# Two evictions of a four-layer model on one core: Delta's second bank from ScalarE to VectorE, and VectorE first at the shared scores bank

## The chip, the cores and the metric

The kernel runs on one core of a Trainium2 chip. The metric is the device time of one execution in microseconds (us), here the median of three. Lower is better. The profile is of one further execution with its own time.

Engines: TensorE (PE, with its weight loads PEld), VectorE (DVE), ScalarE (ACT), GpSimd (POOL) and SyncE (SP), which issues nearly all DMAs. Each has its own queue of instructions.

## The reference

The input is a batch of 8 images of 56 x 56 positions and 192 channels. Four layers follow each other, each as `x = x + layer(group_norm(x))`:

```python
# layer 0: gated Toeplitz mixing along both axes, 576 channels
out = p * (toeplitz_w(q * v, a1) + toeplitz_h(q * v, a2)) @ o_w.T + o_b
# layer 1: 7 x 7 window attention, shifted by 3, 6 heads of 32
attn = softmax((q * hd**-0.5) @ k.T + bias + mask);  out = (attn @ v) @ proj_w.T + proj_b
# layer 2: depthwise 3 x 3 convolution
# layer 3: selective scan over 4 directions, 384 channels, 16 states
delta = softplus(dts + dt_b)
dA = exp(delta * A);  dBu = delta * u * B
h[t] = dA[t] * h[t-1] + dBu[t];  y[t] = sum_n h[t] * C[t] + D * u[t]
```

In layer 3 two directions run along rows (forward and backward) and two along columns. The four results are added, normed over the channels, gated with silu(z) and projected back.

## The kernel before

**Three parts.** The first (to L300) computes the Toeplitz products of all images. The second runs the *front* of image 0 beside the rest of the first. A front is everything from the gate of layer 0 to the deltas of layer 3 of one image, in five stages: `gate` (L448), `attention`, `conv2`, `inner`, `steps`. In the first two parts the instructions are placed by the framework's scheduler. The third part is the scan loop, under a manual schedule: the order in which the program writes the instructions is the order in the queues. It holds the scans of all images and the fronts of images 1 to 7.

**The scan loop.** An image is cut into chunks of 448 positions, 7 for each of the 4 directions, so 28. A chunk has 3 blocks of 128 channels and 8 groups of 2 states, so an image has 28 x 24 = 672 *pairs* (block and group), and the loop runs over 5376 of them. A pair consists of: `inject` (L1059, GpSimd: delta * u times B), `decay` (L1076, ScalarE: two exponentials into a PSUM tile of which there are two), `initial` (L1066) and `keep_state` (L1098, small ScalarE copies), `scan` (L1085, VectorE), `times_c` (L1091, on GpSimd for even groups, on VectorE for odd ones) and `add_up` (L1106, TensorE sums over the states in PSUM). After the last group of a block `sums` (L1116, L1118, VectorE) adds the result to `ysum`. Once the fourth direction has passed a chunk, `finish` (L959 to L1003) norms, gates and projects it.

**Fronts and `finish` beside the scans.** Both are generators. Each `yield` ends a *segment* and tells the planner how many PSUM banks are held across it, how many the next one needs, and sometimes a delay. There are two such banks. After each pair the loop calls `parts.step`, which may resume each generator several times, up to limits. The planner keeps a planned time per engine and adds the cost of every instruction as it writes it. Front costs were logged while image 0's front was written: `Meter` (L46) gives each instruction a base and a cost per element: 0.2 + 0.83e-3 n us on ScalarE, 0.1 + 1.05e-3 n on VectorE, 0.04 + 1.25e-3 n on TensorE; the costs of a segment count one after the other. `Parts.fits` decides whether a segment goes now:

```python
t, at, grace = dict(self.t), entry.ready, 3.0 * entry.waits
for engine, cost in entry.costs[entry.at]:
    if engine == "D" and at > t["D"] + limit["D"] + grace:
        return False
    at = t[engine] = max(t[engine], at) + cost
return all(t[e] <= max(limit[e] + grace, self.t[e]) for e in "AE")
```

The limit of "D" (VectorE) in the loop is 0.2 us. A refusal adds one to `entry.waits`, an admission sets it to 0.

**The deadline.** A chunk's deltas are loaded ahead of it: at block 1, group 0 of the chunk before, which is 16 pairs ahead of the chunk's first pair. For the first chunk of image b these deltas come from image b's own front, so the loop there says

```python
while (b1, slot1 // 2, j1) not in made:
    parts.step(anything, ahead_of)
```

with no limits, until `steps` has made the block. The next front is added as soon as the one before is through.

**The stages that the change touches or that matter here.** In `attention` the loop runs over 8 rows of windows and in each over 4 groups `q` of two windows. For each group: the scores of the six heads in three banks of 196 columns (L614); the third of these banks also takes the product v (L643), 192 columns behind the scores. `biased` (the call lands on L619, VectorE) scales the scores and adds the bias. `nc.scalar.copy(v, pv)` (L645) takes v out of the shared bank. Then the row maximum (L648, VectorE), the exponentials (L651, ScalarE, in two segments of three), the reciprocal (L656, VectorE), the scaling (L659, ScalarE), transposes (L666) and the product with v (L678).

In `inner`, for each of 3 blocks of 128 channels: for 7 tiles a projection with two halves (L840), evicted by ScalarE (L845, L848), one half going to a padded buffer in DRAM; from it the convolution (loads L811, matmuls L869, evictions L879); Silu of both halves over the whole image (L886, with the reload of z's half at L883 and the stores at L888); seven ScalarE copies that turn rows into columns (L892), and a store (L896).

In `steps`, for each direction axis o (columns first) and each of 7 chunks: load (L907), matmul (L918), a ScalarE copy (L920), then for each of 3 blocks two matmuls (L928) into two banks, one bank for each of the two directions s, and their evictions with the bias (L933, ScalarE, 128 x 448); at the end the Softplus of all six at once (L937, 128 x 2688) with a table load ahead of it and one behind it, and the stores (L940).

Of the kernel before, what the change touches and what calls it, by code (L numbers as in the profile page):

```python
# [16 lines left out]
AF = mybir.ActivationFunctionType  # L17
ALU = mybir.AluOpType
# [9 lines left out]
CH = 448  # L28
# [60 lines left out]
def model(ctx: ExitStack, tc: tile.TileContext, a: dict, out: bass.AP):  # L89
    nc = tc.nc  # L90
# [213 lines left out]
    with (  # L304
# [4 lines left out]
        cb2, cb3, dt_b = (load_const(wp, n) for n in ("cb2", "cb3", "dt_b"))  # L309
# [34 lines left out]
        def bank():  # L344
            return ps.tile([128, 512], F32, name="ps_f")
# [6 lines left out]
        bias, bmask, masks = carve(slab, PT_, (NH, WS, 2, WS), (4, 6, PT_), (4, PT_))  # L352
# [175 lines left out]
        def attention(b):  # L528
# [40 lines left out]
            p = bank()  # L569
# [11 lines left out]
            for wh in range(H // WS):  # L581
                x = xs[:, wh % 2]
                yield 0, 0

                for k in range(2):
                    nc.scalar.copy(x[:, k, :, W:], x[:, k, :, :SHIFT])

                    nc.scalar.copy(
                        xw[:, k].rearrange("p q (i j) -> p q i j", i=WS),
                        x[:, k, :, SHIFT:].rearrange("p i (q j) -> p q i j", q=4),  # L590
                    )
                for m in range(4):
                    yield 0, 1
                    p = bank()
                    for k in range(2):
                        nc.tensor.matmul(
                            p[:CP, :n],
                            w_qkv[:, k, m * CP : (m + 1) * CP],
                            xw[:, k].rearrange("p q t -> p (q t)"),
                            start=k == 0,  # L600
                            stop=k == 1,
                        )
                    yield 1, 0
                    nc.scalar.activation(
                        qk[:, m].rearrange("p q t -> p (q t)"), p[:CP, :n], AF.Identity, bias=nb[:CP, m : m + 1]
                    )
                if wh + 1 < H // WS:
                    load_x(wh + 1)
                for q in range(4):
                    kind = 2 * (wh == 7) + (q == 3)  # L610

                    def scores(p, hh, t):
                        row = slice(hh * HD, (hh + 1) * HD)
                        nc.tensor.matmul(  # L614
                            p[:PT_, t * PT_ : (t + 1) * PT_], qk[row, t, q, :], qk[row, 2 + t, q, :], start=True, stop=True
                        )

                    def biased(p, hh):
                        nc.vector.scalar_tensor_tensor(  # L619
                            S[:, 2 * hh : 2 * hh + 2, :],  # L620
                            p[:PT_, : 2 * PT_].rearrange("p (t m) -> p t m", t=2),
                            HD**-0.5,
                            bmask[:, kind, 2 * hh : 2 * hh + 2, :],
                            ALU.mult,
                            ALU.add,
                        )


                    yield 0, 2
                    p0, p1 = bank(), bank()  # L630
                    for t in range(2):
                        scores(p0, 0, t)
                        scores(p1, 1, t)
                    yield 2, 0
                    biased(p0, 0)
                    biased(p1, 1)
                    yield 0, 1
                    p = bank()
                    for t in range(2):
                        scores(p, 2, t)  # L640
                    pv = p[:PT_, 2 * PT_ : 2 * PT_ + C]
                    for k in range(2):
                        nc.tensor.matmul(pv, xw[:, k, q, :], w_qkv[:, k, 2 * C :], start=k == 0, stop=k == 1)  # L643
                    yield 1, 0
                    nc.scalar.copy(v, pv)  # L645
                    biased(p, 2)
                    mx, sm = mxs[:, 0], mxs[:, 1]
                    nc.vector.tensor_reduce(mx, S, axis=AX.X, op=ALU.max, negate=True)  # L648
                    yield 0, 0
                    for e in range(6):  # L650
                        nc.scalar.activation(  # L651
                            S[:, e, :], S[:, e, :], AF.Exp, bias=mx[:, e : e + 1], accum_out=sm[:, e : e + 1]
                        )
                        if e == 2:
                            yield 0, 0
                    nc.vector.reciprocal(sm, sm)  # L656
                    yield 0, 0
                    for e in range(6):
                        nc.scalar.activation(S[:, e, :], S[:, e, :], AF.Copy, scale=sm[:, e : e + 1])  # L659
                        if e == 2:  # L660
                            yield 0, 0
                    for g in range(2):
                        yield 0, 1
                        p = bank()
                        for e in range(3):
                            nc.tensor.transpose(  # L666
                                p[:PT_, e * PT_ : (e + 1) * PT_], S[:, 3 * g + e, :], ident[:PT_, :PT_]
                            )
                        yield 1, 0
                        nc.scalar.copy(  # L670
                            ST[:, 3 * g : 3 * g + 3, :].rearrange("p a m -> p (a m)"), p[:PT_, : 3 * PT_]
                        )
                    yield 0, 1
                    p = bank()
                    for t in range(2):
                        for hh in range(3):
                            h = 3 * t + hh
                            nc.tensor.matmul(  # L678
                                p[hh * HD : (hh + 1) * HD, t * PT_ : (t + 1) * PT_],
                                v[:, h * HD : (h + 1) * HD],  # L680
                                ST[:, 2 * hh + t, :],
                                start=True,
                                stop=True,
                            )
                    yield 1, 0
                    nc.scalar.copy(oT[:, :, q, :], p[:CP, : 2 * PT_].rearrange("p (t m) -> p t m", t=2))
                for m in range(2):
                    yield 0, 1
                    p = bank()
                    for t in range(2):  # L690
                        nc.tensor.matmul(
                            p[:CP, :n],
                            w_pr[:, t, m * CP : (m + 1) * CP],
                            oT[:, t].rearrange("p q (i j) -> p i q j", i=WS),
                            start=t == 0,
                            stop=t == 1,
                        )
                    yield 1, 0
                    pi = p[:CP, :n].rearrange("p (h w) -> p h w", h=WS)
                    for cd, cs in ((slice(0, W - SHIFT), slice(SHIFT, W)), (slice(W - SHIFT, W), slice(0, SHIFT))):  # L700
                        nc.vector.scalar_tensor_tensor(
                            x[:, m, :, cs], pi[:, :, cd], vb[:, m : m + 1], x[:, m, :, cs], ALU.add, ALU.add
                        )
                for i0, i1, h0 in rows(wh):
                    for k in range(2):
                        nc.sync.dma_start(out=image(x2_d[b], k, i0, i1, h0), in_=x[:, k, i0:i1, :W])
# [192 lines left out]
        def steps(b):  # L899

            w_x, xc, rc, dl = carve(slab, 128, (2, ND, 128), (2, ND, CH), (2, CH), (2, ND, CH))
# [9 lines left out]
            for n, (o, j) in enumerate(todo):  # L911
# [4 lines left out]
                p = bank()  # L916
# [5 lines left out]
                for d in range(ND):  # L922
                    yield 0, 2
                    held = []
                    for s in range(2):
                        row = slice(32 * s, 32 * s + R)
                        held.append(bank())
                        nc.tensor.matmul(  # L928
                            held[s][:, :CH], w_dt[row, o, d * 128 : (d + 1) * 128], rc[row, n % 2, :], start=True, stop=True
                        )  # L930
                    yield 2, 0
                    for s in range(2):
                        nc.scalar.activation(  # L933
                            dl[:, s, d, :], held[s][:, :CH], AF.Identity, bias=dt_b[:, 2 * o + s, d : d + 1]
                        )
                yield 0, 0
                nc.scalar.activation(dl, dl, AF.Softplus)  # L937
                usual_functions()
# [487 lines left out]
```

## Time and profile before

| | |
|---|---|
| time, median of 3 runs | 21470.86 us (21421.38 to 21477.67) |
| the profiled execution's own time | 21510.71 us |
| its span, first to last instruction | 21508.5 us |
| busy share of the span | PE 81%, DVE 73%, POOL 70%, ACT 58% |
| first scan of the loop (L1085) | 3423.3 us |
| granted TensorE clock, mean | 0.865 |
| L645 (v out of the shared bank) | 224 in the loop, 319 ns median |
| L933 (delta's evictions) | 588 in the loop |

The page tells busy time by engine, then the span in 40 slices. Up to slice 6 (3423 us) the first two parts run; from there on the loop. The groups by line tell busy time, the mean duration of one instruction and the idle time ahead of them with what ended it. "Windows" gives the same busy time for stretches of the span, or the time and count of a single line in them; as each pair has one scan, that count is the number of pairs. Instructions written for image 0's front and placed by the scheduler all carry the line of the recording helper (L83), so the counts by line of the front's stages are those of images 1 to 7.

### The profile page before, as it was taken

To read this page: it belongs to the slowest core of one execution; us is meant where nothing else is said; L and a number is where in the kernel's file an instruction comes from. 1 tells how busy PE (TensorE), PEld (TensorE's weight loads), DVE (VectorE), ACT (ScalarE), POOL (GpSimd) and SP (SyncE) were. 2 spreads that over 40 slices of the span, in tenths; PEclk is the share of its full clock that TensorE was granted. 3 is DMA by queue.
4 is the path that set the end of the run, shared out by engine and by line. 5 is a ranking of instruction groups with operands and counts; after the bars stand their busy time and mean duration, and the time that the engine had idled before them with its cause. 6 is when DMAs were issued, how large, how long until landed. Compare 5 with 4: busy or idle time off the path is not lost. (4 is left out here: it accounts for less than half of the span.)

```text
span 21508.5 us, 203992 instructions
## 1 busy us (share of the span) xinstructions
PE 17461.0 (81%) x59404; PEld 9086.2 (42%) x59404; DVE 15779.7 (73%) x12469; ACT 12490.5 (58%) x31833; POOL 15095.0 (70%) x9176
## 2 busy tenths in 40 slices
PE   7878678887887789877987788879877888787777
PEld 4845455433443344433543354334433443333333
DVE  2122116996799668977898779867987789789998
ACT  3126113666666566757575657666666667575555
POOL 0000005887788678867897778878887788689999
PEclk9587757998998889888998899889988999888888
DMA  3931676456544755466545654565446554754444
GB/s 88 248 97 39 190 211 181 131 159 213 172 142 134 217 166 152 134 183 199 160 128 172 209 157 138 159 212 170 140 148 214 173 146 132 218 180 147 134 131 128
DMA packets 2566532, 3470.45 MB, mean 161 GB/s; under 512 B 936270, under 2 KB 2518704, under 8 KB 2534578
## 3 DMA queue, kind: packets, MB, share of 16 engines
q1 hardware_dynamic: 2542724, 3340.61, 52.4%
q0 software_dynamic: 15520, 116.14, 1.5%
q8 instruction: 473, 7.75, 0.2%
q14 instruction: 647, 5.30, 0.1%
q10 hardware_dynamic: 7168, 0.65, 0.0%
HBM read 2822.68 MB, written 634.11 MB: 161 GB/s over the span
## 5 line engine op out<-in xcount | busy, mean ns | idle before, releaser
L1106 PE MATMUL ps_y<-hc,ident_sb 128*128 128x448 f32 x21504 | 10003.9, 603 | 828.4 <-POOL hc L1091 750.6
L1059 POOL TENSOR_TENSOR ring<-du,bm 128x896 f32<-128x896 f32 x5376 | 9450.8, 1775 | 745.8 <-ACT ring L1066 383.2
L1076 ACT ACTIVATE ps_a<-delta,A_logs_sb 128x449 f32<-128x449 f32 x10752 | 6859.6, 638 | 354.3 <-DVE ring L1085 97.7
L1106 PEld LDWEIGHTS ps_y<-hc,ident_sb 128*128 128x128 f32 x21504 | 4315.8, 210 | 5154.2 <-issue 3636.4
L1091 POOL TENSOR_TENSOR hc<-ring,cm 128x896 f32<-128x896 f32 x2688 | 4769.2, 1774 | 1930.7 <-DVE ring L1085 922.1
L1085 DVE TENSOR_TENSOR_SCAN ps_a<-ps_a,ring 128x898 f32<-128x898 f32 x2688 | 5428.3, 2019 | 607.8 <-ACT ps_a L1076 558.2
L1085 DVE TENSOR_TENSOR_SCAN ring<-ps_a,ring 128x898 f32<-128x898 f32 x2688 | 5424.1, 2018 | 571.8 <-ACT ps_a L1076 407.1
L1091 DVE TENSOR_TENSOR hc<-ps_a,cm 128x896 f32<-128x896 f32 x2688 | 2935.2, 1092 | 1037.6 <-PE ps_y L1106 808.0
L1098 ACT COPY state<-ps_a 128x2 f32<-128x2 f32 x2687 | 426.5, 159 | 2783.3 <-DVE hc L1091 2775.4
L287 DVE COPY tzx<-ps_tz 112x448 f32<-112x448 f32 x432 | 269.9, 625 | 1442.5 <-PE ps_tz L281 1292.4
L281 PE MATMUL ps_tz<-tzx,tm 112*112 112x112 f32 x4608 | 1031.1, 406 | 344.7 <-DMA tm<-ext 295.9
L295 POOL DMA_DIRECT2D o<-tzx x192 | 97.3, 513 | 1579.6 <-DVE tzx L287 1341.0
L281 PEld LDWEIGHTS ps_tz<-tzx,tm 112*112 112x112 f32 x4608 | 1021.8, 319 | 385.7 <-issue 381.9
L1066 ACT COPY ring<-state 128x2 f32<-128x2 f32 x4608 | 823.0, 179 | 532.2 <-POOL hc L1091 531.1
L666 PE MATMUL ps_f<-ident_sb,slab 98*98 98x98 f32 x1344 | 336.5, 325 | 602.9 <-ACT slab L659 602.7
L1098 ACT COPY state<-ring 128x2 f32<-128x2 f32 x2688 | 504.1, 188 | 489.6 <-DVE ring L1085 476.2
L1042 POOL TENSOR_TENSOR du<-delta,xcd 128x448 f32<-128x448 f32 x672 | 659.8, 982 | 20.0 <-DMA slab<-in_w_p_dram 19.6
L83 PE MATMUL ps_f<-slab 96*32 96x448 f32 (+7 forms) x2432 | 588.4, 548 | 75.9 <-DMA slab<-pad 55.9
L234 PE MATMUL ps_qv<-wqv,xn 96*128 96x384 f32 (+1 forms) x1200 | 530.3, 525 | 135.6 <-ACT sl L236 68.0
L666 PEld LDWEIGHTS ps_f<-ident_sb,slab 98*98 98x98 f32 x1344 | 202.5, 157 | 1017.5 <-ACT slab L659 798.5
L503 PE MATMUL ps_f<-ident_sb,slab 112*96 112x112 f32 x4704 | 534.7, 268 | 99.7 <-DVE slab L511 49.8
L503 PEld LDWEIGHTS ps_f<-ident_sb,slab 112*96 112x96 f32 x4704 | 513.1, 170 | 239.0 <-issue 121.6
(221 smaller groups left out, 16398.9 us busy)
## 6 DMA issues: line engine op xcount, KB each, us to landing
bm<-bc SPq DMA_DIRECT2D x1792, 448.0 KB
cm<-bc SPq DMA_DIRECT2D x1792, 448.0 KB
xcd<-xc SPq DMA_DIRECT2D x840, 224.0 KB
dl<-slab SPq DMA_DIRECT2D x224, 672.0 KB
delta<-dl SPq DMA_DIRECT2D x224, 672.0 KB
slab<-pad SPq DMA_DIRECT2D x504, 232.0 KB
tzx<-qv SPq DMA_DIRECT2D x192, 588.0 KB
o<-tzx POOLq DMA_DIRECT2D x192, 588.0 KB, 14.2
```

The costliest lines, as they stand in the source:

```text
L83: return f(*args, **kw)
L281: nc.tensor.matmul(po[:, c, :], t[:, :, c2 + c], x[:, :, c1 + c2 + c], start=True, stop=True)
L503: nc.tensor.matmul(p[:CP, t * TT : (t + 1) * TT], ot[:, n % 2, i, t, c % 2 * CP : c % 2 * CP + CP], ident[:TT, :TT], start=i == 0, stop=i ...
L666: nc.tensor.transpose(p[:PT_, e * PT_ : (e + 1) * PT_], S[:, 3 * g + e, :], ident[:PT_, :PT_])
L1042: nc.gpsimd.tensor_mul(du[:, 0, :], deltas[i][:, d, 1 : CH + 1], xcs.pop((i, d)))
L1059: nc.gpsimd.tensor_mul(hs[:, :, tokens(i)[0]], dus[i, d].to_broadcast([128, NG, CH]), bms[i, k])
L1066: nc.scalar.copy(in_ring(g)[:, :, tokens(i)[1]], src)
L1076: nc.scalar.activation(dA[:, n, :], deltas[i][:, d, at : at + CH + 1], AF.Exp, scale=negA[:, slot, d, c : c + 1])
L1085: nc.vector.tensor_tensor_scan(h, dA, hs, 0.0, ALU.mult, ALU.add)
L1091: (nc.gpsimd if on_pool(d, k) else nc.vector).tensor_mul(hc, h[:, :, tokens(i)[0]], cms[i, k])
L1098: nc.scalar.copy(states[i][:, d, NG * k : NG * k + NG], h[:, :, tokens(i)[2]])
L1106: nc.tensor.matmul(yps[i, d][:, :CH], ident, hcs[g][:, n, :], start=k + n == 0, stop=k + n == NP + NG - 2)
```

## The change

In `attention` the copy of v and the third call of `biased` change places: VectorE now reads the shared bank first, then ScalarE, then VectorE reduces. In `steps` the loop over the two directions is written out: the first direction's bank is still evicted by ScalarE (now L932), the second one's by VectorE with `tensor_scalar` (L933), which adds the bias as a scalar per partition. Over 8 images that is 336 evictions in 112 blocks of 3. No buffer, DMA or matmul is changed. The costs that `Meter` logs change with the instructions, and so do the decisions of the planner and of the scheduler ahead of the loop.

```diff
@@ -642,8 +642,8 @@
                     for k in range(2):
                         nc.tensor.matmul(pv, xw[:, k, q, :], w_qkv[:, k, 2 * C :], start=k == 0, stop=k == 1)
                     yield 1, 0
+                    biased(p, 2)
                     nc.scalar.copy(v, pv)
-                    biased(p, 2)
                     mx, sm = mxs[:, 0], mxs[:, 1]
                     nc.vector.tensor_reduce(mx, S, axis=AX.X, op=ALU.max, negate=True)
                     yield 0, 0
@@ -929,10 +929,10 @@
                             held[s][:, :CH], w_dt[row, o, d * 128 : (d + 1) * 128], rc[row, n % 2, :], start=True, stop=True
                         )
                     yield 2, 0
-                    for s in range(2):
-                        nc.scalar.activation(
-                            dl[:, s, d, :], held[s][:, :CH], AF.Identity, bias=dt_b[:, 2 * o + s, d : d + 1]
-                        )
+                    nc.scalar.activation(dl[:, 0, d, :], held[0][:, :CH], AF.Identity, bias=dt_b[:, 2 * o, d : d + 1])
+                    nc.vector.tensor_scalar(
+                        dl[:, 1, d, :], held[1][:, :CH], dt_b[:, 2 * o + 1, d : d + 1], None, ALU.add
+                    )
                 yield 0, 0
                 nc.scalar.activation(dl, dl, AF.Softplus)
                 usual_functions()
```

## The prediction

> **What bounds the kernel now.** The page's chain of work is useless here (every share is 0%), so I read the table of windows, the windows of the scan line alone (L1085, whose count is the number of pairs), the waits of VectorE, the groups by line, and the timeline of ScalarE and SyncE at one place.
>
> ```profile
> 20000.00:21000.00 1000.00, 731.85 (x1476) 315.33 (x1477) 957.23 (x602) 557.65 (x1479) 998.81 (x600) 0.86 0.43 140
> 8411.00:9198.00 787.00, 657.60 (x2318) 324.98 (x2317) 733.36 (x609) 566.79 (x1793) 697.92 (x417) 0.90 0.41 123
> 18402.00:18826.00 424.00, 327.28 (x1136) 143.46 (x1136) 297.58 (x188) 253.36 (x563) 309.40 (x184) 0.87 0.73 224
> 18826.00:19113.00 287.00, 249.38 (x595) 102.56 (x596) 215.52 (x137) 240.63 (x470) 227.68 (x137) 0.86 0.61 207
> ```
>
> Columns: window, us, then PE, PEld, DVE, ACT, POOL busy. Row 1 is the last image, with no front stage beside it: GpSimd is full. Row 2 is an attention stage: VectorE 93% busy, it is the bound. Rows 3 and 4 are inner and steps of the last front: no engine is full, waits between engines cost the time.
>
> ```profile
> 20000.00:21000.00 1000.00, 735.52 (x370) 0.86 0.43 140
> 8411.00:9198.00 787.00, 513.23 (x256) 0.90 0.41 123
> 3423.00:19113.00 15690.00, 9096.34 (x4534) 0.90 0.56 168
> 19113.00:21508.00 2395.00, 1678.67 (x843) 0.88 0.42 136
> 18717.00:18848.00 131.00, 69.75 (x35) 0.87 0.63 196
> 18797.00:18848.00 51.00, 24.71 (x13) 0.73 0.40 147
> ```
>
> Columns: window, us, VectorE's time in L1085 and the number of scans, granted clock, DMA share, GB/s. 370 scans in 1000 us are the bare pace, 2.70 us a pair. Attention runs at 787/256 = 3.07. Seven fronts took 15690 us and 4534 pairs, 648 pairs a front, though an image has 672: the fronts now run ahead of the scans by 24 pairs an image. That slack is what this change spends.
>
> **Part 1, attention.** No instruction is added: 224 copies L645 (319 ns) and 224 biases L619 (352 ns) swap places in the loop stage. What moves is the plan. A step of the planner admits a segment only if each VectorE operation in it is ready within 0.2 us of VectorE's planned time, plus 3 us for each refusal so far. Before, the segment is copy (A), bias (D), reduce (D). Now it is bias, copy, reduce. In the plan the copy starts when the bias ends and takes 0.2 + 192 x 0.83e-3 = 0.36 us, so the reduce is ready 0.36 us after VectorE's time: more than 0.2, and the first offer is always refused. The built order (no times in it) shows the outcome: a group of two windows took 6 pairs and now takes 8, and an attention stage's 1344/7 exponentials span 305 pairs and not 244. A front so needs 61 pairs more: 648 + 61 = 709, and an image has 672.
>
> The built order also shows what then happens. Scanning image b may not begin before the first delta block of b exists; 16 pairs before the image's end the kernel empties the front's remaining segments into the queues, with no scan between them. Before, the first delta block stood in the queues ahead of that point every time (at pair 550 of 656, at 1202 of 1328, and so on). After, ScalarE's queue shows 33 front instructions in one place, five times (ahead of pairs 2000, 2672, 3344, 4016, 4688): six evictions L845/L848, seven L879, two Silu L886 with their four table loads, seven copies L892, then L920, three evictions L932 and the Softplus L937 with two loads. Ahead of pair 1328 there is a shorter one, from the copies L892 on. VectorE's next scan stands behind the three new evictions of that block, so it waits for the whole chain.
>
> **What one forced chain costs.** The same instructions lie between 18717 and 18848 us in the last front, there with 35 scans among them. From the timeline of SyncE and that of ScalarE in that stretch (start, duration, engine, line; in brackets the idle time and what ended it):
>
> ```profile
> 18784.31 0.34 SPq L883 DMA_DIRECT2D slab<-zr  x1
> 18801.36 0.33 SPq L888 DMA_DIRECT2D z<-slab  x1
> 18815.41 0.32 SPq L896 DMA_DIRECT2D xc<-slab  x1
> ```
>
> ```profile
> 18798.52 2.82 ACT L886 ACTIVATE slab<-slab 128x3136 f32<-128x3136 f32 x1
> 18806.52 1.06 ACT L892 COPY slab<-slab 128x448 f32<-128x448 f32 x1 [2.35 <-DMA z<-slab]
> 18830.93 0.53 ACT L920 COPY slab<-ps_f 128x448 f32<-128x448 f32 x1 [7.39 <-PE ps_f L918]
> ```
>
> Most of it is a chain through DRAM that scans do not lengthen. Alone I take: six tiles of L840 at 1.67 us of TensorE, 10 to 13; writing the pad and reading it back, 10 to 11.6 (18735.8 to 18747.5 here); six more convolution tiles, 24 to 37 (18747.5 to 18784.3); to the end of the second Silu 14 to 16 (its input is fetched at 18784.3, it ends at 18801.3); the store of z ahead of the copies 5.1; seven copies at 0.84, 6; store, reload and L918 14 to 16 (18815.4 to 18831.5); three delta pairs 7 to 10; Softplus with its two table loads 5.0. Sum 95 to 120, taken 107, less some 4 us in which scans issued earlier still run: 103. What the same stretch costs today is 131 - 35 x 2.70 = 36. So one forced chain costs 103 - 36 = 67 us net, five cost 335. The shorter one: copies, reload, deltas, Softplus are 6 + 15 + 8 + 5 = 34 and a few of waiting, say 40, against 51 - 13 x 2.70 = 16 today: +24. Together **+359**.
>
> Does attention give some back? It is thinner by 61 pairs. Without give-back it takes 787 + 61 x 2.70 = 952 us. Its floor is VectorE's own work, 733 + 61 x 957/370 = 891. So 0 to 61 a front. Its waits of VectorE in that stage sum to some 40 us, 24 of them the reciprocal waiting for the exponentials, and that wait stays. One is added: the copy (ScalarE) now waits for the bias (VectorE), with the first exponentials, the state copy and the next decay queued behind it, and a scan waiting for that decay. The exponentials wait for the reduce anyway, which follows the bias, so the copy adds only its own 0.32 us to the 0.77 of the reduce. I take 3 a front, -21 in all.
>
> **Part 2, delta.** 294 evictions in the loop (42 a front) and 42 ahead of it leave ScalarE.
>
> ```profile
> L933 ACT ACTIVATE slab<-ps_f,dt_b_sb 128x448 f32<-128x448 f32 x588 | 341.1, 628 | 169.3 <-PE ps_f L928 161.2 <-DMA dl<-slab 6.4
> L511 DVE TENSOR_TENSOR slab<-slab,ps_f 96x448 f32<-96x448 f32 x294 | 177.9, 605 | 44.2 <-PE ps_f L503 43.7
> L791 DVE SCALAR_TENSOR_TENSOR slab<-ps_f,cb_sb,slab 96x448 f32<-96x448 f32 x98 | 66.3, 677 | 197.0 <-PE ps_f L780 189.0 <-DMA cm<-bc 8.0
> ```
>
> ```profile
> DVE ring L1085 <- ACT ps_a L1076: 35.4, 11, 3.4
> ```
>
> The first three are groups by line (busy us and mean ns, then idle time before and what ended it), the last is a wait of VectorE between 18826 and 19113 us (sum, times, longest). One eviction costs ScalarE 0.58 of busy time (628 ns, overlapped). The trace has no such VectorE form; its 448-wide readers of a bank lie at 605 and 677 ns, and the plain one is nearer: 0.6. A front so takes 42 x 0.6 = 25 us off one engine and puts 25 on the other. In steps (row 4 above) VectorE idles 287 - 216 = 71, and the last row shows why: the scan waits for decays behind the 5 us Softplus block, which stays. Bounds: -25 a front if the decays come that much earlier, +48 if VectorE pays the 25 and waits for TensorE as ScalarE did (161 us over 7 fronts is 23 each). ScalarE is the busier (84% against 75%), VectorE stands on the chain: I take 0.
>
> The trace's rows weigh against a rule here. The Trainium skill, "Perfetto Trace Analysis", Optimizing Scalar/DVE Operations, gives VectorE about 125 ns of overhead on a PSUM access and ScalarE about 51; by it each moved eviction is 0.07 us dearer, 22 us in all if none were hidden. The rows show no such gap. For the change speaks the Trainium skill, "TensorEngine Tiling (Array Packing)", PSUM Bottleneck, which says to evict with both engines; by it alone the estimate would be 7 x 25 = 175 us faster. The refusal in the plan is outside either rule.
>
> The section ahead of the scans (to 3423 us) is reordered too; nothing added, taken at 0, bounds 30 either way.
>
> **Sum.** 359 - 21 + 0 = +338 on the profiled span of 21508.5. That execution took 21510.7 us, 0.19% over the median 21470.86. In those terms 21470.86 + 338 = 21809, taken as **21805 us** (1.6% slower).
>
> **Rivals.**
> *Not slower: attention falls to VectorE's floor.* The thinner stage gives back up to 61 us a front, 427 us; it decides from 359/7 = 51 on. At the floor the time is 21470 + 359 - 427 = 21400. For it: no more 12 exponentials between two decays, at most 6. Against it: GpSimd would then be at 856/891 = 96%, and the waits it would have to lose are only some 54 us of 787.
> *ScalarE's relief decides.* The 44 us (35.4 of even groups above, 8.4 of odd ones) that scans wait for decays in a steps stage vanish: -308, total about 21500; same. Against it: the Softplus block causes them.
> *VectorE pays in full.* +48 a front, 336 more: 22140. For it: its queue is in order, and a scan waits behind each eviction.
> *That the change does not reach the code* is excluded by the built order, which has 336 VectorE evictions.
>
> **Numbers.** Forecast 0.76, VectorE pays 0.10, relief decides 0.08 (same), attention's floor 0.06 (half of it below 21406). The forecast's own range: chains of 95 to 120 make 5 x 12 = 60 either way, steps +-20 a front 140, attention -100; 21560 to 22040 takes these in and most of the way to the dearer rival. About 0.3% (64 us) is what a measurement can tell from no change: faster 0.04, same 0.09, slower 0.87.
>
> **What would show it.** In the changed profile: five gaps of some 100 us without a scan, one per image from the third on; attention 900 to 950 us long; steps some 280 us, with scans behind L933. Wrong if the gaps are under 60 us, or if the images between them run faster than today.

## The result, and the profile after

| | before | after |
|---|---|---|
| median of four runs each on one chip, us | 21474.26 | 21601.54 (21591.23 to 21611.45) |
| ratio | | 1.0065, 95% interval 1.0048 to 1.0082 |
| span of the profiled execution, us | 21508.5 | 21604.1 |
| busy: PE, DVE, POOL, ACT | 81, 73, 70, 58% | 81, 74, 70, 57% |

The change makes the kernel 0.65% slower, 127 us. The forecast had 338 us. Its sign was right and the time lies in its range, but the size is off by more than a factor of two.

The forced chains are there. VectorE's timeline around one of them, in the changed kernel (start, duration, engine, line; in brackets the idle time and what ended it):

```profile
10142.93 2.03 DVE L1085 TENSOR_TENSOR_SCAN ps_a<-ps_a,ring 128x898 f32<-128x898 f32 x1
10145.05 1.09 DVE L1091 TENSOR_TENSOR hc<-ps_a,cm 128x896 f32<-128x896 f32 x1
10235.54 0.68 DVE L933 TENSOR_SCALAR slab<-ps_f,dt_b_sb 128x448 f32<-128x448 f32 x1 [89.40 <-PE ps_f L928]
10237.84 0.68 DVE L933 TENSOR_SCALAR slab<-ps_f,dt_b_sb 128x448 f32<-128x448 f32 x1 [1.61 <-PE ps_f L928]
10240.47 0.68 DVE L933 TENSOR_SCALAR slab<-ps_f,dt_b_sb 128x448 f32<-128x448 f32 x1 [1.95 <-PE ps_f L928]
10241.07 2.02 DVE L1085 TENSOR_TENSOR_SCAN ring<-ps_a,ring 128x898 f32<-128x898 f32 x1
```

From one scan to the next 98.1 us pass, with the three evictions of the new block ahead of the second scan, as forecast. The other gaps of this kind last 97.6, 97.3, 98.7 and 98.2 us, and the short one lasts 41.0. ScalarE's timeline in the same stretch shows the links, each a wait for another engine or a transfer:

```profile
10168.32 0.63 ACT L879 ACTIVATE slab<-ps_f,cb_sb 128x448 f32<-128x448 f32 x1 [11.42 <-PE ps_f L869]
...
10197.30 0.63 ACT L879 ACTIVATE slab<-ps_f,cb_sb 128x448 f32<-128x448 f32 x1 [6.25 <-PE ps_f L869]
...
10204.66 2.82 ACT L886 ACTIVATE slab<-slab 128x3136 f32<-128x3136 f32 x1
...
10212.72 5.96 ACT L892 COPY slab<-slab 128x448 f32<-128x448 f32 x7 [3.94 <-DMA z<-slab]
10233.81 0.53 ACT L920 COPY slab<-ps_f 128x448 f32<-128x448 f32 x1 [15.12 <-PE ps_f L918]
```

The pad's way through DRAM takes 11.4 us, seven convolution tiles 30, the Silus to their end 10, the store ahead of the copies and the copies 11, the next reload with its matmul 15.

The windows of all engines (length; PE, PEld, DVE, ACT, POOL busy; granted clock; DMA share; GB/s) show an attention stage, the inner stage that holds this chain, the steps stage after it, and the chain alone:

```profile
8664.00:9584.00 920.00, 755.43 (x2570) 372.97 (x2569) 884.11 (x712) 660.02 (x2042) 865.92 (x519) 0.92 0.41 129
9775.00:10229.00 454.00, 332.25 (x1232) 158.49 (x1231) 254.90 (x168) 244.53 (x523) 277.30 (x169) 0.85 0.67 203
10230.00:10554.00 324.00, 279.24 (x672) 120.26 (x670) 255.56 (x189) 235.50 (x466) 247.53 (x150) 0.86 0.59 199
10143.00:10241.00 98.00, 47.86 (x221) 17.26 (x222) 4.95 (x6) 30.26 (x37) 3.11 (x2) 0.66 0.53 161
```

In the chain no engine is busy for more than half of the time, and GpSimd, the pace of the bare scans, does 3 us of work in 98. In the attention stage shown VectorE idles 36 us, where it idled 54 in the one of before (the means of all seven are 41 and 49). The same stretches for the scans alone:

```profile
8664.00:9584.00 920.00, 636.36 (x319) 0.92 0.41 129
3420.00:19910.00 16490.00, 9575.20 (x4776) 0.89 0.55 166
19910.00:21604.00 1694.00, 1197.16 (x601) 0.88 0.41 134
```

Attention now takes 319 pairs and 920 us: 2.88 us a pair, where it was 3.07. All seven fronts take 4776 pairs, 682 a front and not 648.

For the sums below each stage of a front is cut at one instruction near its start (the first L486, L586, L746, L840 and L918), and its **excess** is its time less 2.70 us for each pair in it, summed over the seven fronts. `tail` is what follows the last front's last instruction.

| stage | before: us / pairs / excess | after: us / pairs / excess | change of the excess |
|---|---|---|---|
| gate | 3423.6 / 973 / 796 | 3003.9 / 918 / 525 | -271 |
| attention | 5509.8 / 1805 / 636 | 6500.2 / 2235 / 466 | -171 |
| conv2 | 1179.7 / 278 / 429 | 1256.4 / 280 / 500 | +71 |
| inner | 2979.3 / 790 / 846 | 3257.8 / 697 / 1376 | +530 |
| steps | 2586.4 / 685 / 737 | 2461.0 / 643 / 725 | -12 |
| tail | 2395.5 / 842 / 122 | 1693.7 / 600 / 74 | -48 |

These add up to +99, the section ahead of the loop to -3, together the +96 between the spans. The loss is in `inner`, which holds the chains. The question is what gave back some 200 us.

### The profile page after: what moved, and what is told of

It is laid out like the page before. It is cut to its first block, busy times and chain, and to the rows that moved or that the text cites. A ratio compares the mean times of both kernels' runs of the same rounds, so it can differ in the third digit from the quotient of the medians.

```text
span 21604.1 us, 204934 instructions
## 1 busy us (share of the span) xinstructions
PE 17467.7 (81%) x59404; PEld 9102.8 (42%) x59404; DVE 15954.3 (74%) x12805; ACT 12323.1 (57%) x31502; POOL 15080.3 (70%) x9176
## 5 line engine op out<-in xcount | busy, mean ns | idle before, releaser
L1106 PE MATMUL ps_y<-hc,ident_sb 128*128 128x448 f32 x21504 | 9899.2, 599 | 604.0 <-POOL hc L1091 563.3
L1076 ACT ACTIVATE ps_a<-delta,A_logs_sb 128x449 f32<-128x449 f32 x10752 | 6856.6, 638 | 308.5 <-DVE ring L1085 51.5
L295 POOL DMA_DIRECT2D o<-tzx x192 | 97.3, 513 | 1565.1 <-DVE tzx L287 1381.7
L928 PE MATMUL ps_f<-slab,w_dt_sb 12*128 12x448 f32 x1176 | 453.9, 717 | 229.1 <-ACT slab L920 179.8
L988 POOL TENSOR_TENSOR slab_f<-slab_f 128x672 f32<-128x672 f32 x110 | 151.0, 1373 | 691.0 <-ACT slab_f L984 667.4
```

The source lines that it names most:

```text
L1076: nc.scalar.activation(dA[:, n, :], deltas[i][:, d, at : at + CH + 1], AF.Exp, scale=negA[:, slot, d, c : c + 1])
L1106: nc.tensor.matmul(yps[i, d][:, :CH], ident, hcs[g][:, n, :], start=k + n == 0, stop=k + n == NP + NG - 2)
```

## The experiments

**The theory** was the forecast's: the order of two attention instructions changes the logged costs, the plan made from them spreads attention over more pairs, and the front is then late for its image's first deltas. **The rivals**: the order itself costs (the shared bank is read by VectorE first and ScalarE after it), or Delta's evictions on VectorE do.

### Each part alone

Delta alone, then the swap alone:

```diff
-                    for s in range(2):
-                        nc.scalar.activation(dl[:, s, d, :], ..., bias=dt_b[:, 2 * o + s, d : d + 1])
+                    nc.scalar.activation(dl[:, 0, d, :], ..., bias=dt_b[:, 2 * o, d : d + 1])
+                    nc.vector.tensor_scalar(dl[:, 1, d, :], ..., dt_b[:, 2 * o + 1, d : d + 1], None, ALU.add)
```

> The eviction of the second direction's bank by VectorE alone; the attention order of before. In the built order no forced chain is left and a front takes about 645 pairs. Theory A (the attention swap, by way of the plan, makes all of the +127 us): 0 +-30 us against before, ratio 0.9985 to 1.0015. Rival B (VectorE pays for the evictions: about 0.68 us each and its waits for TensorE, 48 us a front): +150 to +340 us, ratio over 1.007. Rival D (ScalarE's relief is worth its 25 us a front and was hidden by the chains): -100 to -175 us, ratio under 0.995.

```diff
+                    biased(p, 2)
                     nc.scalar.copy(v, pv)
-                    biased(p, 2)
```

> The attention swap alone; both banks evicted by ScalarE as before. Theory A: five gaps of 95 to 100 us without a scan and one of some 45, attention at 2.89 us a pair over 319 pairs, and a time of +100 to +160 us against before. Rival B: near 0. Rival D: +230 to +300 us, because the relief of ScalarE is missing.

Delta alone: 21456.51 us against 21502.45, ratio 0.998 (0.9971 to 0.9989), 46 us faster, and no gap. The swap alone: 21690.74, ratio 1.0087 (1.0074 to 1.0101), 188 us slower, with gaps of 46.1, 101.3, 99.6, 101.3, 99.5 and 101.7 us. The two add up to +142, the whole change measures +127. So all of the loss is the swap's, and the chains come from it alone.

### The order or the plan

The swap in images 1 to 7 only: the costs are logged in image 0's front, so the plan stays as before, while the loop's instructions are swapped.

```diff
+                    if b > 0:
+                        biased(p, 2)
                     nc.scalar.copy(v, pv)
-                    biased(p, 2)
+                    if not (b > 0):
+                        biased(p, 2)
```

> The swap in the instructions of images 1 to 7 only; the costs are logged from image 0 with the order of before, so that the plan (6 pairs per group of two windows) is that of before, pair by pair. Theory A (only the plan matters): 0 +-20 us against before. Rival C (the copy's new wait for VectorE, with exponentials and the next decay behind it, costs by itself): 0.5 to 0.9 us for each of 224 groups, +110 to +200 us, and more idle time of VectorE ahead of its scans in attention.

The reverse, the swap in image 0 only: the loop's instructions are those of before, the plan is that of the swap.

```diff
+                    if b == 0:
+                        biased(p, 2)
                     nc.scalar.copy(v, pv)
-                    biased(p, 2)
+                    if not (b == 0):
+                        biased(p, 2)
```

> The reverse: the instructions of images 1 to 7 keep the order of before, but the costs are logged from an image 0 with the swapped order, so that the plan is that of swap_only (8 pairs per group, forced chains). Theory A: the time of swap_only within 20 us, with the same six gaps. Rival C: the time of before plus 0 to 30 us.

The swap without its plan: 21566.65 us, ratio 1.003 (1.0019 to 1.0042), +64 us, and no gap. The plan without the swap: 21717.05, ratio 1.0101 (1.0087 to 1.0114), +215 us, with gaps of 45.9, 103.0, 98.8, 102.0, 99.9 and 103.4. So the plan makes the chains, whatever the order of the two instructions in the loop. The order has a price of its own under the old plan. Waits of VectorE (what waits, for what; us, times, longest us), first before, then the swap without its plan, whose lines L654 and L659 are L651 and L656 of before:

```profile
DVE mxs L656 <- ACT slab L651: 140.2, 183, 0.9
```

```profile
DVE mxs L659 <- ACT slab L654: 220.3, 221, 1.3
```

The reciprocal waits 80 us longer for the exponentials, and attention's excess rises from 636 to 712. Under the new plan this wait is 102.4 us with the swap and 102.4 without it: the order adds no wait there, and the intervals of the two ratios (1.0074 to 1.0101 and 1.0087 to 1.0114) overlap. That fits 64 and 215 not adding up to 188.

The gaps came as theory A said. The times of these four kernels all lie outside its ranges, by 6 to 44 us: it had nothing for Delta's 46 or for the order's 64, and the swap alone is dearer than it said.

### Fewer pairs for attention, without the chains

The whole change, but the swap only in the first rows of windows, so that fewer groups are spread (shown for four of the eight rows; the other kernels of this kind have 6, 3 and 2 in place of 4):

```diff
+                    if wh < 4:
+                        biased(p, 2)
                     nc.scalar.copy(v, pv)
-                    biased(p, 2)
+                    if wh >= 4:
+                        biased(p, 2)
```

> The changed kernel with the swap in the first four of eight rows of windows only: 4 rows at 8 pairs per group, 4 at 6. In the built order a front then takes some 676 pairs and just meets its deadline (first delta block at pair 4681 of 4688 in the last image); no forced chain is left. Theory A2 (the swap's thinner plan gives back about 24 us a front in attention, the chains take some 46 us net per image more than that): half of the 171 us of attention's excess back, -85, the -46 of the delta part, and no chain: -90 to -170 us against before, ratio 0.992 to 0.996. Rival E (the give-back does not exist; what fell in attention is only moved to other stages): -46 +-30, ratio 0.9965 to 0.9995.

> The same with six rows swapped. The built order has two full chains (34 ScalarE instructions in one place) and two short ones (19). Theory A2: gaps of some 98 us twice and some 45 us twice, which cost 286 us less the 100 that the same work costs interleaved, +186; attention -128, delta -46: 0 to +40 us. Rival F (the chains cost nothing net, since what they do is no longer to be done beside the scans): -170 us or more.

> The same with three rows swapped, so that the fronts keep 50 pairs of slack. Theory A2: three eighths of 171, -64, and -46: -80 to -140 us, 10 to 30 us slower than some4. Rival E: as some4, -46 +-30.

Four rows: 21400.13 us against 21493.58, ratio 0.9957 (0.9944 to 0.997), no gaps. Three rows: 21396.73, ratio 0.9952 (0.994 to 0.9965), no gaps. Six rows: 21517.77, ratio 1.001 (1.0001 to 1.0019), with gaps of 72.6, 46.4, 73.2 and 46.2 (the two long ones were expected at some 98). So these two kernels, with a thinner attention and without chains, are *faster* than before; one with two rows, below, is not. In `some4` the excess of attention is 569 against 636 before, and of `inner` 1056 against the 1376 of after.

Three rows without Delta's part tell what Delta gives in this version:

```diff
+                    if wh < 3:
+                        biased(p, 2)
                     nc.scalar.copy(v, pv)
-                    biased(p, 2)
+                    if wh >= 3:
+                        biased(p, 2)
```

> The swap in three of eight rows alone, with both of Delta's banks evicted by ScalarE as before. If the two parts add up (some3 was -97 us, delta_only -46): about -50 us, ratio 0.9965 to 0.999. If the gain of some3 is all the plan's: -90 to -110. If the delta part pays only beside the thinner plan: 0.

21428.82 us against 21493.31, ratio 0.9971 (0.9958 to 0.9983). The intervals of 0.9971 and 0.9952 overlap a little; the difference, some 40 us, fits the 46 of Delta alone. But Delta's part also changes the logged costs (alone it takes a front from 647 to 644 pairs), and no run separates its instructions from its plan, as was done for the swap.

### Both of Delta's banks on VectorE

Before's attention, and both evictions on VectorE:

```diff
                     for s in range(2):
-                        nc.scalar.activation(dl[:, s, d, :], ..., AF.Identity, bias=...)
+                        nc.vector.tensor_scalar(dl[:, s, d, :], ..., dt_b[...], None, ALU.add)
```

> The attention order of before, and both of Delta's banks evicted by VectorE: twice the moved work, 84 evictions of 0.68 us a front. If ScalarE's relief is what gained the 46 us of delta_only, twice the move gives -60 to -100 us. Rival B2 (one bank each lets the two evictions run at the same time; both on VectorE put them in line again, and scans behind them): the gain is gone, -20 to +80 us.

21597.01 us, ratio 1.0045 (1.0033 to 1.0058), 103 us slower than before and more than the rival allowed. One bank gained 0.2%, the second loses 0.65% of the time. `steps` has 104 us more excess than with one bank, though VectorE's evictions wait for their matmuls for only 10.5 us in all. So the evictions' own waits are not the loss. That the work queued behind them on VectorE pays is a candidate, and so is the plan, which changed too (642 pairs a front); no run shows either by itself.

### The same instructions in another place

With the swap in two rows the kernel was expected to gain like the one with three:

> The changed kernel with the swap in two rows only, 663 pairs a front. If attention's give-back goes with the number of thinned rows: between delta_only (-46) and some3 (-97), about -75 us. If what some3 gained comes from where finish and the fronts' stages meet (fronts at a fixed place in every image once they take 672 pairs), it is as fast as some3, as its fronts also settle at 672 pairs from the third on.

It lost: 21644.19 us against 21493.31, ratio 1.0069 (1.0056 to 1.0081), with no gap. Its excess in `steps` is 1047, against 830 with three rows. The next idea was that `steps` now falls beside another part of `finish`. The same kernel with its first front begun 30 pairs later moves all places and changes no instruction:

```diff
-                if ahead_of not in parts.clients and b_next < B:
+                if ahead_of not in parts.clients and b_next < B and g >= 30:
```

> some2 with one thing changed: the first front of the loop starts at pair 30 and not at pair 0. In the built order its fronts stand from the third on at the very pairs at which some3's stand (gate at 2055, first Softplus at 1945), 41 pairs later than in some2. Theory G (where in the image the steps stage meets finish sets some 200 us; some2 has all of its steps beside finish): as some3 or little slower, -50 to -100 us against before. Rival H (two thinned rows are dear by themselves, the place does not matter): as some2, +120 to +180 us.

21223.27 us against 21467.36, ratio **0.9886 (0.9873 to 0.9899)**: the fastest of all kernels here, 244 us ahead of before, where 50 to 100 were expected. One of the steps stages each, in windows of all engines, first two rows, then two rows and the later start:

```profile
12275.00:12704.00 429.00, 353.07 (x872) 164.27 (x871) 311.91 (x229) 282.50 (x576) 314.48 (x190) 0.85 0.54 176
```

```profile
12244.00:12624.00 380.00, 336.23 (x870) 155.71 (x869) 316.15 (x232) 281.60 (x581) 322.10 (x196) 0.90 0.62 203
```

Nearly the same instructions (229 and 232 of VectorE, 576 and 581 of ScalarE) take 429 and 380 us, and the busiest engine, TensorE, is at 82 and 88%. Over the loop the excess of `steps` is 1047 and 710. The granted clock differs as well, 0.85 and 0.90; TensorE's busy time falls by 17 of the 49 us, so the clock can be a part of the difference and not all of it, and whether it is cause or consequence isn't shown. The wait that differs most is one of TensorE, again first two rows, then the later start:

```profile
PE ps_f L996 <- POOL slab_f L991: 540.8, 101, 7.8
```

```profile
PE ps_f L996 <- POOL slab_f L991: 251.3, 61, 9.8
```

It is `finish`'s projection (L993 in before), waiting for the product that GpSimd makes last (L988 in before). Every matmul of the front and of the scans is queued behind it.

Holding the fronts in the kernel with Delta alone, 50 pairs past each image's start, tests whether a place is worth as much without a thinner attention:

```diff
-                if ahead_of not in parts.clients and b_next < B:
+                if ahead_of not in parts.clients and b_next < B and g >= 672 * (b_next - 1) + 50:
```

> delta_only, with each front held back until pair 50 of its image; no row of attention is thinned. The first Softplus of a front then stands at 1949, 2621 and so on, as in some3. Theory G alone (place, not thinning, made some3 faster than delta_only): -97 +-25 us against before. If thinning attention gives back by itself, some3 must stay faster: -30 to -60 us here. If holding fronts back costs: above -20.

21427.38 us, ratio 0.9979 (0.997 to 0.9989), the same as Delta alone at its own place. `gate` lost 252 us of excess (766 to 514), `steps` and `inner` got 409 more (696 to 939, 843 to 1009), the other stages lost the rest. This place brought nothing, and by the expectation the gain of three rows over Delta alone is then the thinner attention's own.

The pair at which a stage starts doesn't settle the time either. From the fourth front of the loop on, a front's first Softplus starts after 600 pairs of the image that is being scanned in the kernel with two rows and the later start, after 602 with three rows and after 604 with the held fronts; these three take 244, 97 and 40 us less than before. With two rows and no later start it is after 556.

### Is it the wait for GpSimd's product?

If TensorE's wait at the head of its queue is the cost, a delay between product and projection must save it, in any kernel. In `finish`, for two rows, for before and for after:

```diff
                 nc.gpsimd.tensor_mul(yu, yu, sq)
-                yield 0, 1
+                yield 0, 1, 4.0
```

> some2 with one number changed: in finish, the planner counts 4 us more between GpSimd's last product (L988 of the kernel before) and the output matmul that reads it, so that TensorE gets this matmul later. No instruction is changed, the fronts stay within 13 pairs of some2's places. Theory G2 (what made some2 slow is TensorE standing at that matmul with add_up queued behind it): the wait falls from 541 to under 200 us and the time by 150 to 350 us, to 0 to -200 against before. Rival I (the wait only goes with the place of the stages, which is the cause): still +80 to +180.

> The kernel before with the same number. Theory G2: the wait falls from 307 to some 100 us and the time by 80 to 180 us. Rival I: 0 +-40.

> The changed kernel with the same number. Theory G2: the wait falls from 180 to some 60 us, the time by 40 to 110 us from +127, so +20 to +90 against before; against before_fin it is then dearer by 150 to 250 us, more than the 127 of the change, because the part that the shifted places gave is gone. Rival I: +127 +-30.

The same wait, first of two rows with the delay, then of before and of before with the delay:

```profile
PE ps_f L996 <- POOL slab_f L991: 77.5, 27, 5.5
```

```profile
PE ps_f L993 <- POOL slab_f L988: 307.3, 90, 7.4
```

```profile
PE ps_f L993 <- POOL slab_f L988: 89.9, 37, 5.5
```

In the kernel with two rows it holds: the wait falls from 541 to 78 us, and the ratio to before from 1.0069 to 0.9942 (0.9929 to 0.9954; 21374.88 us against 21516.33), with 331 us less excess in `steps` (1047 to 716). In before it fails: the wait falls by 217 us, and the time stays (21500.34, ratio 0.9999, 0.999 to 1.0007). In after it fails too: 180 to 118 us, and the time is 21655.67, ratio 1.0074 (1.0061 to 1.0087), with gaps no shorter (46.4 and 101.6 to 105.0). So in that one kernel the loss goes with this wait; its fronts moved too, the first Softplus from 556 to 565 pairs into the image, so that wait and place are not wholly separated. The wait doesn't explain what places are worth in before and after. Nor does it elsewhere: it is 446 us with the held fronts and 233 with Delta alone, and these two take the same time.

## Why the prediction was right in sign and wrong in size

**Chains, +359: right, at most 11% too dear.** All six came, five of some 98 us and a shorter one of 41. Less what the same stretches cost today by the forecast (36 each, and 16) they are 489.9 - 5 x 36 + 41.0 - 16 = 335. Taken as the difference of `inner` between after and the kernel with four rows they are 1376 - 1056 = 320. Of the links only the Silus lay clearly outside their bounds, 10 us from the fetch of their input on and not 14 to 16. The Softplus lies behind the gap, not in it: the scan starts 0.1 us ahead of it, and the next one pays.

```profile
10241.22 1.28 ACT L937 ACT_TABLE_LOAD   x1 [0.48 <-DVE slab L933]
```

```profile
10247.73 2.04 DVE L1085 TENSOR_TENSOR_SCAN ps_a<-ps_a,ring 128x898 f32<-128x898 f32 x1 [4.64 <-ACT ps_a L1076]
```

With these 4.6 the chain shown costs 102.7, where the forecast had 103. That the plan and not the new order makes the chains was shown by the pair of kernels with one of them each. The reason given in the plan holds, and is part of it: by the program's own rules a group of two windows is refused 3.2 times in the mean after the change and 1.3 times before. The first refusal after the change is always the reduce's, 0.36 us against 0.2, as forecast; in nearly every group one more is the reciprocal's, also against VectorE's limit, and one is for ScalarE's limit at the scaling.

**Attention's give-back, "I take 3 a front, -21 in all": this step failed.** It measured -171, some 24 a front (928.6 us a front, 61 pairs more than the 787.1 of before, and 61 x 2.70 = 165). The kernel with the swap alone shows the same without Delta: by the same cuts its attention gives back 150 us, its chains, counted as above, cost 354, all the rest is -13, and their sum over the loop, +191, stands beside the +188 between the medians.

The step had the bounds right, 0 to 61, and took a value near the end at which nothing is given back. What it had wrong most is the price of an added pair in this stage, GpSimd's 2.70 us. VectorE is the bound here: over the seven stages it is busy for 5167 of 5510 us before and for 6215 of 6500 after. So 430 added pairs cost it 1048 us, 2.44 each, and at 2.70 they would be 1161: that is 113 of the 171. The swap alone and the plan alone have 2.44 and 2.47. The forecast's floor had 957/370 = 2.59 for it, which would be 7 of these 16 us a front; why it is still less no run shows. The other 58 are idle time of VectorE, 343 us before and 285 after. The largest part of that is the wait that was to stay, the reciprocal's, which went from 140 to 106 us over the loop:

```profile
DVE mxs L656 <- ACT slab L651: 105.6, 174, 0.6
```

The forecast itself had a reason for it, as an argument for its rival: after the change at most six exponentials stand between two decays, where twelve did. No run tests that by itself. The rival "attention falls to VectorE's floor" would have needed 51 a front to decide; it did not come, but the truth lay between the two. (Its 856 us for GpSimd adds VectorE's 2.59 us a pair; with GpSimd's 2.70 it is 863, 97% of the 891.)

A part of the 171 can be the place and not the thinner plan: with 273 pairs a front each, attention's excess is 597 with two rows and 541 with the later start, and it is 658 with Delta alone and 610 with the held fronts.

**Places, 0: not priced.** The rest of the table, -271 + 71 - 12 - 48 and the 210 of `inner` that is also there without chains, comes to -50. With the chains counted by their gaps (335) it is -66, against the -13 of the swap alone, which has no part of Delta's: so most of it may be Delta's -46, and the places net to little while their terms are large. These terms follow the plan and not the order: the excess of `gate` is 788 for the swap without its plan and 561 for the plan without the swap. That `gate` gains what `inner` loses agrees with the fronts' being moved against `finish`. Why a place is worth what it is in these two kernels **stays open**: the wait for GpSimd's product, the one candidate tried, is not it. The marker "wrong if the images between them run faster than today" points at these steps too. They do run faster: less its chain, an image's 672 pairs take 82 to 114 us less than before in four of five images (in the last one 44 more, as before had its last front through by then). By that marker the size was wrong.

**Delta, 0 with bounds -25 to +48 a front: right in size.** It is -46 in all, 7 a front. "ScalarE's relief decides" (-308) and "VectorE pays in full" (+336) are both excluded for one bank; with both banks on VectorE the loss goes the second rival's way, with 103 us. The group of the new evictions, by line and form (busy us, mean ns, idle before and what ended it):

```profile
L933 DVE TENSOR_SCALAR slab<-ps_f,dt_b_sb 128x448 f32<-128x448 f32 x294 | 198.6, 675 | 530.6 <-PE ps_f L928 526.5 <-DMA dl<-slab 3.2 <-PE ps_y L1106 0.5
L932 ACT ACTIVATE slab<-ps_f,dt_b_sb 128x448 f32<-128x448 f32 x294 | 184.9, 629 | 183.5 <-PE ps_f L928 180.5 <-DMA dl<-slab 2.6
```

The forecast took 0.6 us; it is 0.675, the dearer of the two rows that it chose between. Of the 526.5 us of waiting 499.9 stand in the six chains (93.0, 92.1, 92.4, 93.5, 93.1 and 35.8) and are theirs, not Delta's.

The Trainium skill, "Perfetto Trace Analysis", Optimizing Scalar/DVE Operations, puts VectorE's overhead on a PSUM access at about 125 ns and ScalarE's at about 51. The rows agree in direction: 675 against 629 ns is 46 dearer, where the page's figures differ by 74; the rows are whole evictions and not the overhead alone, so the size is not tested here. The forecast's remark that the rows show no such gap was wrong. The kernel with Delta alone gains all the same: in it the scans wait 107 us less for their decays (L1076; 965 us before, 859 after), which fits ScalarE's relief, though no run shows that this is the cause.

**The markers.** Five gaps of some 100 us without a scan came, and attention is 929 us long in the mean (900 to 950 forecast). `steps` is 352 us in the mean and not "some 280": that number came from the last front alone, and before it was 369 in the mean already. The row was not typical.

## What to carry to other kernels

Where a program places work by logged costs, the order of two instructions is also an input of that plan: to price it, run the old order under the new plan and the new order under the old one. Work that is moved into a stage is priced by the engine that bounds this stage, and not by the pace elsewhere; and a bound from 0 to 61 with a reason on each side should not be taken at 3. When small edits move the time by a per cent in both directions, compare the same instructions at another place before a cause is given to any of them.

## What the runs showed of the hardware that was not expected

- The granted clock of TensorE is 0.65 to 0.68 in the five chains and 0.58 in the short one, against 0.92 in the attention stage ahead of the one shown. The forecast priced the chain from a stretch at 0.87, and it came out no longer.
- One matmul waits for GpSimd at the head of TensorE's queue. With a later place for it the time of one kernel fell by 1.3% (the wait went from 541 to 78 us) and that of another did not change (307 to 90 us). The sum of a wait does not tell what it costs.
- A pair added to a stage in which VectorE is busy for 94 to 96% cost VectorE 2.44 us, where a pair of the last image, with GpSimd full, takes 2.70.
- Two readers of one bank in the other order cost 64 us over 224 groups under one plan, and added no wait under another (the reciprocal waits 102.4 us in both).
